# The last group of softmax weights, the last unit and the last rows in another form

## The chip, the cores and the metric

The kernel runs on one core of a Trainium2 chip. The metric is the device time of the whole launch in microseconds (us). The engines named here are TensorE (PE in the profile; PEld is its weight load), VectorE (DVE), ScalarE (ACT), GpSimd (POOL) and SyncE (SP). SP, and in this kernel ScalarE, also issue DMA transfers, which 16 DMA engines carry out. SBUF is the on-chip memory of 128 partitions; PSUM is the memory that TensorE writes.

## The reference

Eight batches of 1024 rows of 128 numbers go through one layer: a layer norm, an attention of eight query heads that share one key and one value projection, a linear "FFN", and the residual.

```
xn = _layernorm(x)                          # x: 8 x 1024 x 128, float32
Q = einsum('bnd,hdk->bhnk', xn, proj_q);  K = einsum('bmd,dk->bmk', xn, proj_k)
V = einsum('bmd,dv->bmv', xn, proj_v)
weights = softmax(einsum('bhnk,bmk->bhnm', Q, K))
Y = einsum('bhnv,hdv->bnd', einsum('bhnm,bmv->bhnv', weights, V), proj_o)
out = x + Y + sum over 8 experts of (xn @ w1[e]) @ w2[e]
```

The FFN has no activation between its two products, so the kernel folds it into one 128 x 128 matrix, `wf`.

## The kernel before

**Units and blocks.** A unit u is one head of one batch: 64 units. A unit has eight blocks of 128 queries; a block is numbered i, 0 to 511, and one pass of the main loop handles one block. The loop writes out the order on every engine by hand; no scheduler moves anything.

**One block.** `logits(i)` (L286 to L338) makes a 128 x 1024 block of logits in PSUM with four matmuls, in one of two buffers of the pool `ps_sc`; VectorE takes the row maximum (`nmax`, L335) and ScalarE the exponential with its sum (`e`, L338). `divide(i)` has VectorE take the reciprocal (L342) and ScalarE multiply (L343).

**Turning the weights.** The product with the values needs the weights with the keys on the partitions. `weights_t(i - 1)` has VectorE turn 32 x 32 squares (L365) into a tile `turned` that holds four blocks, a group. When a group is full, `move_blocks` sends its 4 x 4 pieces of 32 partitions, 128 KB each, to their partitions with 16 DMAs on SP's queue (L381). A unit has two groups, `g0` and `g1`. The last group of the last unit (blocks 508 to 511) goes another way: `weights_t_pe` transposes each block on TensorE (L354) into a `ps_sc` buffer, and ScalarE and VectorE copy one half each into `g1` (L356); nothing of it is moved by DMA.

**Seven products for eight.** The product of weights and values is done on 2 x 2 blocks (query groups by key halves) in a Strassen-Winograd form with seven products. Of the weights, x1 and x2 are the key halves of `g0`, y1 and y2 of `g1`, and four sums are made: F1 = x1 + x2 (`sum_early`, L391), then X1 = y1 - x1 (L396), X2 = F1 - y1 (L397) and F4 = y2 - X2 (L399) in `sums_late`; X1 and X2 overwrite x1 and x2 in place. All run on GpSimd, save that the last unit's `sums_late` runs on VectorE. F1 and F4 live in two alternating buffers of the tag `f`.

**Pairs.** `pair(u, j)`, j from 0 to 13, is two matmuls at L423 on the two halves of TensorE's columns, 64 wide and 512 long. Pairs 0 and 1 use x2 before it is overwritten and add to accumulator 3 (P4). Pairs 2 to 5 use y1 and y2 as they are (accumulator 0), pairs 6 to 9 use X1 and F1 (accumulator 1), pairs 10 to 13 use X2 and F4 (accumulator 2). The list `jobs` holds all pairs in order and, for each batch, four matmuls of the FFN (L446); the loop takes `PAIRS = (2, 2, 1, 2)` of them in turn from block 12 on, so the products run about a unit and a half behind the logits, and go on for 12 passes after the last block (`NS + LAG`).

**Rows.** When a batch's products are done, `collect` adds the halves of the four accumulators into `c1`, `p1`, `c2`, `y0` and `y1` (twelve steps, L478 to L504; accumulator 3 enters c1 first). For the last batch, steps 6 to 11 come behind everything else; then `rows_out_pe` transposes y0 and y1 back to rows on TensorE (L538), `finish_pe` adds x on VectorE (L542), half by half, and SP stores each half (L543).

Of the kernel before, what the change touches and what calls it, by code (L numbers as in the profile page):

```python
# [9 lines left out]
F32 = mybir.dt.float32  # L10
# [7 lines left out]
def kernel(  # L18
# [53 lines left out]
    GN = 4  # L72
# [62 lines left out]
    def scratch(tag, size, pool=work, bufs=None):  # L135
        return pool.tile([P, size], F32, tag=tag, name=f"scratch_{tag}", bufs=bufs)
# [46 lines left out]
    wqk = const.tile([P, H, P], F32, tag="wqk", name="wqk")  # L183
    wvo = const.tile([P, H, P], F32, tag="wvo", name="wvo")
    wf = const.tile([P, P], F32, tag="wf", name="wf")
    moments = const.tile([P, B, NB, 2], F32, tag="moments", name="moments")
    rstd = const.tile([P, B, NB], F32, tag="rstd", name="rstd")

# [133 lines left out]

    sums, es, turned, g0s, g1s, f1s, f4s = {}, {}, {}, {}, {}, {}, {}

    def logits(i):
        u, n = divmod(i, NB)
        pl = slot(f"pl_{i}")
        for g in range(2):  # L330
            both_halves(
                pl[:, ts(g, GS)], qTs[u][:, ts(n, P)], xnTs[u // H][:, ts(g, GS)]
            )
        nmax = small.tile([P, 1], F32, tag="nmax", name=f"nmax_{i}")
        nc.vector.reduce_max(nmax, pl, AX.X, negate=True)  # L335
        sums[i] = small.tile([P, 1], F32, tag="sums", name=f"sums_{i}")
        es[i] = work.tile([P, S], F32, tag="e", name=f"e_{i}")
        nc.scalar.activation(es[i], pl, AF.Exp, bias=nmax, accum_out=sums[i])  # L338

    def divide(i):  # L340
        rinv = small.tile([P, 1], F32, tag="rinv", name=f"rinv_{i}")
        nc.vector.reciprocal(rinv, sums.pop(i))  # L342
        nc.scalar.mul(es[i], es[i], rinv)  # L343

    def weights_t_pe(i):

        k, j = divmod(i, GN)
        u = k // 2
        if j == 0:
            g1s[u] = work.tile([P, NQ, NB, GN, Q], F32, tag="turned", name=f"g1_{u}")  # L350
        e = es.pop(i)
        pt = slot(f"pe_{i}")
        for c in range(NB):
            nc.tensor.transpose(pt[:, ts(c, P)], e[:, ts(c, P)], ident)  # L354
        for a, copy in enumerate((nc.scalar.copy, nc.vector.tensor_copy)):
            copy(  # L356
                g1s[u][:, :, ts(a, HC), j].rearrange("p r c q -> p c r q"),
                pt[:, ts(a, GS)].rearrange("p (c r q) -> p c r q", c=HC, q=Q),
            )

    def weights_t(i):
        k, j = divmod(i, GN)
        if j == 0:
# [8 lines left out]
    def move_blocks(k):  # L372
        src = turned.pop(k)
        u, g = divmod(k, 2)
        dst = work.tile(
            [P, NQ, NB, GN, Q], F32, tag=f"g{g}", name=f"g{g}_{u}", bufs=2 - g
        )
        (g1s if g else g0s)[u] = dst
        for r in range(NQ):
            for d in range(NQ):  # L380
                nc.sync.dma_start(dst[ts(d, Q), r], src[ts(r, Q), d])  # L381

    def key_half(t, a):
        return t[:, :, ts(a, HC)].rearrange("p r c t q -> p r c (t q)")
# [8 lines left out]
    def sums_late(u, engine):  # L393
        x1, x2 = key_half(g0s[u], 0), key_half(g0s[u], 1)
        y1, y2 = key_half(g1s[u], 0), key_half(g1s[u], 1)
        engine.tensor_sub(x1, y1, x1)  # L396
        engine.tensor_sub(x2, f1s[u], y1)  # L397
        f4s[u] = form("f4", u)
        engine.tensor_sub(f4s[u], y2, x2)  # L399

    accs = {}

    def pair(u, j):

        b, h = divmod(u, H)
        vf = vfs[u // GN]
        x1, x2 = key_half(g0s[u], 0), key_half(g0s[u], 1)
        if j < 2:
            acc, first, last = 3, 0, 1
            halves = ((x2, 3, j), (x2, 3, j + 2))  # L410
        else:
            acc, c = divmod(j - 2, HC)
            first, last = acc * HC + 2, acc * HC + 5
            if acc == 0:
                halves = ((key_half(g1s[u], 1), 1, c), (key_half(g1s[u], 0), 0, c))
            elif acc == 1:
                halves = ((x1, 6, c), (f1s[u], 4, c))
            else:
                halves = ((x2, 5, c), (f4s[u], 2, c))
        if h == 0 and j == first:  # L420
            accs[b, acc] = ps_acc.tile([P, GS], F32, tag=f"acc{acc}", name=f"acc{acc}_{b}")
        for half, (w, f, c) in enumerate(halves):
            nc.tensor.matmul(  # L423
                accs[b, acc][ts(half, HP)],
                lhsT=vf[:, u % GN, f, c, :],
                rhs=w[:, :, c, :],
                start=(h == 0 and j == first),
                stop=(h == H - 1 and j == last),
            )

    row_diffs, ends, ys, outs, pos = {}, {}, {}, {}, {}

    def row_diff(b):
        row_diffs[b] = late.tile([P, GS], F32, tag="diff", name=f"diff_{b}")
# [17 lines left out]
    def in_order(t):  # L454
        return t.rearrange("p (r t q) -> p t r q", r=NQ, q=Q)

    def by_query(t):
        return t.rearrange("p (t r q) -> p t r q", t=GN, q=Q)
# [70 lines left out]
            nc.sync.dma_start(r, xs[b][p, c])  # L529
        del xs[b]  # L530

    def rows_out_pe(b, g):

        if g == 0:
            pos[b] = slot(f"po_{b}")
        y = ends[b][2 + g]
        for c in range(GN):
            nc.tensor.transpose(pos[b][:, ts(g * GN + c, P)], y[:, ts(c, P)], ident)  # L538

    def finish_pe(b, g):  # L540
        c = ts(g, GN)
        nc.vector.tensor_add(xs[b][:, c], blocks(pos[b])[:, c], xs[b][:, c])  # L542
        nc.sync.dma_start(chunked(out[b])[:, c], xs[b][:, c])  # L543

# [58 lines left out]
    }  # L603

    PAIRS = (2, 2, 1, 2)
    COLLECT = {0: [0], 2: [1], 3: [2, 3], 4: [4], 6: [5], 7: [6, 7, 8], 8: [9], 10: [10], 11: [11]}

    FIRST_ROWS = 4
# [13 lines left out]
            jobs.extend((ffn, u // H, k) for k in range(2))  # L622
    jobs.reverse()

    for i in range(NS + LAG):
        m = i % GN
        if i < NS:
            logits(i)
        for task in early.get(i, ()):
            task()  # L630
        if 0 <= i - 1 < NS - GN:
            weights_t(i - 1)
        if i < NS:
            divide(i)


        v, n = divmod(i - LAG, NB)
        if n == 6 and 0 <= v + 1 < B * H:
            sum_early(v + 1)


        if i >= LAG:
            for _ in range(min(PAIRS[m] + (n == 0 and v % H == H // 2 + 1) * 2, len(jobs))):
                job, *args = jobs.pop()
                job(*args)
            if n == 0 and v < B * H:
                sums_late(v, nc.gpsimd if v + 1 < B * H else nc.vector)
        if NS - GN <= i - 1 < NS:
            weights_t_pe(i - 1)

        if i % NB == 0 and i > 0 and i // NB + 1 < B * H:
            queries(i // NB + 1)
        if i % NB == GN and i >= LAG:
            s, r = divmod(i + 20, 32)
            if s < 2 * B:
                values(s, r // NB)


        if i == 4:
            load_x(0)  # L660
        for b in range(1, B):
            r = i - FIRST_ROWS if b == 1 else i - (b - 2) * H * NB - 44
            if r in ROWS:
                ROWS[r](b)
            r = i - 20 if b == 1 else i - (b - 1) * H * NB
            if b == B - 1:
                if r == 3:
                    xn_t(b)
            elif r in (0, 4, 8, 12):
                if r == 0:  # L670
                    turn_rows(b)
                move_rows(b, r // 4)
        b, r = divmod(i - 23, H * NB)
        if r == 0 and b < B:
            row_diff(b)


        b, r = divmod(i - 69, H * NB)
        if 0 <= b < B and (b < B - 1 or r < 7):
# [12 lines left out]

    b = B - 1
    for n in (6, 7, 8, 9):
        collect(b, n)
    rows_out_pe(b, 0)
    for n in (10, 11):
        collect(b, n)
    rows_out_pe(b, 1)
    for g in range(2):  # L700
        finish_pe(b, g)
    del xs[b], pos[b], ends[b], ys[b]
    assert not jobs and not ends and not xs and not es


# [34 lines left out]
```

## Time and profile before

| what | us |
|---|---|
| median of 3 runs | 1933.43 (1933.08 to 1933.53) |
| the profiled execution, whole | 1931.35 |
| its span, first to last instruction | 1929.6 |
| PE busy in the span | 1917.4 (99%) |
| VectorE, ScalarE, GpSimd busy | 1397.4, 1358.2, 1406.3 |
| chain that ended last: PE | 87% of the span |
| matmuls of pairs, L423 (g and f, 592 ns each) | 852.2 + 490.7 busy |
| matmuls of logits, L286 pl (593 ns each) | 967.0 busy |
| moves `g<-turned`: 2032 DMAs of 128 KB | 2.4 from issue to landing |

Times of matmuls overlap, so their sum is more than the span. In a row of the timeline the first number is the start in us from the span's start, the second the duration; "x8" counts instructions, and the bracket tells how long the engine was idle before and what released it. A matmul in float32 appears as two records, so a pair is four records and a block of logits eight.

### The profile page before, as it was taken

To read this page: it belongs to the slowest core of one execution; us is meant where nothing else is said; L and a number is where in the kernel's file an instruction comes from. 1 tells how busy PE (TensorE), PEld (TensorE's weight loads), DVE (VectorE), ACT (ScalarE), POOL (GpSimd) and SP (SyncE) were. 2 spreads that over 40 slices of the span, in tenths; PEclk is the share of its full clock that TensorE was granted. 3 is DMA by queue.
4 is the path that set the end of the run, shared out by engine and by line. 5 is a ranking of instruction groups with operands and counts; after the bars stand their busy time and mean duration, and the time that the engine had idled before them with its cause. 6 is when DMAs were issued, how large, how long until landed. Compare 5 with 4: busy or idle time off the path is not lost.

```text
span 1929.6 us, 26694 instructions
## 1 busy us (share of the span) xinstructions
PE 1917.4 (99%) x8966; PEld 650.8 (34%) x8966; DVE 1397.4 (72%) x1775; ACT 1358.2 (70%) x1824; POOL 1406.3 (73%) x588
## 2 busy tenths in 40 slices
PE   9999999999999999999999999999999999999998
PEld 4433333333333333333333333333333333333333
DVE  5767778776786777777777777776777776687775
ACT  6667777777777777767777777776777776777763
POOL 2777776787777786877867778768777687677773
PEclk9999999999999999999999999999999999999999
DMA  7566666766766766677667676666765667567673
GB/s 189 131 154 153 153 139 155 158 155 155 156 153 144 172 155 149 145 159 171 142 149 156 155 171 143 156 149 149 183 143 132 149 152 169 131 148 157 144 170 82
DMA packets 137208, 292.96 MB, mean 152 GB/s; under 512 B 36464, under 2 KB 70000, under 8 KB 137072
## 3 DMA queue, kind: packets, MB, share of 16 engines
q1 hardware_dynamic: 135872, 290.67, 67.1%
q8 instruction: 72, 1.18, 0.3%
q10 hardware_dynamic: 1200, 0.59, 0.1%
q14 instruction: 64, 0.52, 0.1%
HBM read 13.76 MB, written 4.19 MB: 9 GB/s over the span
## 4 chain that ended last, share of the span: by engine, by line
PE 87%; DVE 4%; POOL 2%; ACT 2%; SPq 2%; DMA 1%; issue 1%; POOLq 0%; DVEq 0%
PE pl L286 41%; PE acc L423 34%; PE pq L286 5%; PE pv L286 5%; DVE nmax L335 2%; SPq L381 2%; ACT e L338 1%; DMA g<-turned 1%; DVE turned L365 1%; PE acc L446 1%; POOL g L396 1%; POOL g L397 1%; POOL f L399 1%; ACT e L343 1%; PE pwf L216 0%
## 5 line engine op out<-in xcount | busy, mean ns | idle before, releaser
L286 PE MATMUL pl<-xnT,qT 128*64 128x512 f32 x4096 | 967.0, 593 | 1.4 <-ACT e L338 1.0
L335 DVE TENSOR_REDUCE nmax<-pl 128x1 f32<-128x1024 f32 x512 | 626.4, 1223 | 422.1 <-PE pl L286 421.4
L338 ACT ACTIVATE e<-pl,nmax 128x1024 f32<-128x1024 f32 x512 | 570.6, 1115 | 413.6 <-DVE nmax L335 413.5
L423 PE MATMUL acc<-g,vf 128*64 128x512 f32 x2560 | 852.2, 592 | 0.0
L343 ACT ACTIVATE e<-e,rinv 128x1024 f32<-128x1024 f32 x512 | 588.1, 1149 | 115.7 <-DVE rinv L342 115.6
L365 DVE STREAM_TRANSPOSE turned<-e 128x1024 f32<-128x1024 f32 x508 | 628.7, 1238 | 10.3
L423 PE MATMUL acc<-f,vf 128*64 128x512 f32 x1024 | 490.7, 592 | 0.0
L286 PEld LDWEIGHTS pl<-xnT,qT 128*64 128x64 f32 x4096 | 291.9, 137 | 584.7 <-issue 534.4
L396 POOL TENSOR_TENSOR g<-g,g 128x2048 f32<-128x2048 f32 x63 | 287.1, 4557 | 270.3 <-DMA g<-turned 150.8
L423 PEld LDWEIGHTS acc<-g,vf 128*64 128x64 f32 x2560 | 250.5, 137 | 510.7 <-issue 506.2
L391 POOL TENSOR_TENSOR f<-g 128x2048 f32<-128x2048 f32 x64 | 291.7, 4557 | 177.6 <-PE acc L423 95.8
L399 POOL TENSOR_TENSOR f<-g,g 128x2048 f32<-128x2048 f32 x63 | 287.6, 4564 | 4.9
L397 POOL TENSOR_TENSOR g<-f,g 128x2048 f32<-128x2048 f32 x63 | 287.1, 4557 | 0.6 <-PE acc L423 0.6
L423 PEld LDWEIGHTS acc<-f,vf 128*64 128x64 f32 x1024 | 140.1, 137 | 0.0
L286 PE MATMUL pq<-xnT,wqk 128*64 128x512 f32 x512 | 121.2, 592 | 0.7 <-ACT xnT L281 0.7
L286 PE MATMUL pv<-wvo,xnT 128*64 128x512 f32 x512 | 120.9, 593 | 0.0
L342 DVE RECIPROCAL rinv<-sums 128x1 f32<-128x1 f32 x512 | 83.7, 164 | 48.3 <-ACT e L338 5.1
L338 ACT ACTIVATION_READ_ACCUMULATOR e<-pl,nmax 128x1 f32 x512 | 98.4, 192 | 0.0
L318 POOL TENSOR_TENSOR vf<-vf 128x256 f32<-128x256 f32 x64 | 47.1, 735 | 34.8 <-ACT vf L317 34.8
L298 ACT COPY qT<-pq 128x1024 f32<-128x1024 f32 (+1 forms) x66 | 63.9, 968 | 0.9 <-PE pq L286 0.7
L286 PEld LDWEIGHTS pq<-xnT,wqk 128*64 128x64 f32 x512 | 36.6, 137 | 73.0 <-issue 71.4
L286 PEld LDWEIGHTS pv<-wvo,xnT 128*64 128x64 f32 x512 | 36.4, 137 | 71.5 <-issue 69.3
(84 smaller groups left out, 529.1 us busy)
## 6 DMA issues: line engine op xcount, KB each, us to landing
g<-turned SPq DMA_DIRECT2D x2032, 128.0 KB, 2.4
xn<-in_L_attn_x_dram SPq DMA_DIRECT2D x7, 512.0 KB, 4.6
out<-yt SPq DMA_DIRECT2D x112, 32.0 KB, 1.9
x<-in_L_attn_x_dram SPq DMA_DIRECT2D x7, 512.0 KB, 4.3
xnT<-xnt SPq DMA_DIRECT2D x96, 32.0 KB, 1.9
out_dram<-x SPq DMA_DIRECT2D x6, 512.0 KB, 5.4
scratch_g<-in_L_ffn_w_dram SPq DMA_DIRECT2D x1, 2048.0 KB, 10.4
x<-in_L_attn_x_dram SPq DMA_DIRECT2D x2, 256.0 KB, 3.9
```

The lines of the kernel that those rows point to most:

```text
L286: nc.tensor.matmul(dst[r], lhsT=lhsT[:, r], rhs=rhs, start=True, stop=True)
L298: nc.scalar.copy(qTs[u][:, cols[0] * GS : (cols[-1] + 1) * GS], pq)
L335: nc.vector.reduce_max(nmax, pl, AX.X, negate=True)
L338: nc.scalar.activation(es[i], pl, AF.Exp, bias=nmax, accum_out=sums[i])
L342: nc.vector.reciprocal(rinv, sums.pop(i))
L343: nc.scalar.mul(es[i], es[i], rinv)
L365: nc.vector.transpose(turned[k].rearrange("p k c t q -> p c k t q")[:, :, :, j, :], es.pop(i).rearrange("p (c k q) -> p c k q", k=NQ, q=Q),)
L391: nc.gpsimd.tensor_add(f1s[u], key_half(g0s[u], 0), key_half(g0s[u], 1))
L396: engine.tensor_sub(x1, y1, x1)
L397: engine.tensor_sub(x2, f1s[u], y1)
L399: engine.tensor_sub(f4s[u], y2, x2)
L423: nc.tensor.matmul(accs[b, acc][ts(half, HP)], lhsT=vf[:, u % GN, f, c, :], rhs=w[:, :, c, :], start=(h == 0 and j == first), stop=(h == H ...
```

## The change

- The last group (blocks 508 to 511) is turned by VectorE like all others, and `weights_t_pe` is gone. Its 16 moves are issued half by ScalarE's queue and half by SP's, alternating by the destination; they go into a free buffer of the tag `vf` instead of a `g1` buffer.
- In the last four passes of the loop `PAIRS_LAST = (2, 1, 1, 0)` takes four pairs in place of seven: three pairs come after the last logits instead of between them. The loop ends with the last block; the rest of the pairs of unit 62 follow it.
- The last unit's pairs run in the order 0, 2 to 5, 6 to 9, 10 to 13, 1. So that x2 is still there for pair 1, the last unit's X2 goes into a buffer of its own (`f2s`, in a `g0` buffer).
- The last batch's rows are put together by `last_rows` in an order of its own, with accumulators 0 to 2 alone: two copies on ScalarE and eight adds on VectorE. Accumulator 3 (P4) is copied to SBUF by ScalarE (`d4`) and added on TensorE: the rows are transposed by plain matmuls with the identity, and for the first four chunks a second matmul adds P4's two halves with `fold`, two 64 x 64 identities one above the other. `fold` is made by two GpSimd copies at the start.
- The second half of the last store is issued on ScalarE's queue.

```diff
+    fold = const.tile([P, HP], F32, tag="fold", name="fold")
+    for half in (lo, hi):
+        nc.gpsimd.tensor_copy(fold[half], ident[half, half])
...
-    def weights_t_pe(i):
...
     def move_blocks(k):
         src = turned.pop(k)
         u, g = divmod(k, 2)
-        dst = work.tile(
-            [P, NQ, NB, GN, Q], F32, tag=f"g{g}", name=f"g{g}_{u}", bufs=2 - g
-        )
+        queues = (nc.sync,)
+        if k < 2 * B * H - 1:
...
+        else:
+            queues = nc.scalar, nc.sync
+            dst = scratch("vf", VF, batch)[:, :TURNED].rearrange(
+                "p (r c t q) -> p r c t q", r=NQ, c=NB, q=Q
+            )
         (g1s if g else g0s)[u] = dst
         for r in range(NQ):
             for d in range(NQ):
-                nc.sync.dma_start(dst[ts(d, Q), r], src[ts(r, Q), d])
+                queues[d % len(queues)].dma_start(dst[ts(d, Q), r], src[ts(r, Q), d])
...
     def sums_late(u, engine):
...
+        f2s[u] = x2
+        if u == B * H - 1:
+            f2s[u] = scratch("g0", TURNED)[:, : TURNED // 2].rearrange(
+                "p (r c x) -> p r c x", r=NQ, c=HC
+            )
         engine.tensor_sub(x1, y1, x1)
-        engine.tensor_sub(x2, f1s[u], y1)
+        engine.tensor_sub(f2s[u], f1s[u], y1)
         f4s[u] = form("f4", u)
-        engine.tensor_sub(f4s[u], y2, x2)
+        engine.tensor_sub(f4s[u], y2, f2s[u])
...
+    def last_rows(b, jobs):
...
+        run(0, 1)
+        run(2, 6)
+        nc.scalar.copy(p1[lo], bot(0))
+        nc.scalar.copy(p1[hi], bot(0))
+        add(y1[lo], top(0), p1[lo])
+        run(6, 10)
+        add(c1[lo], top(1), p1[lo])
+        add(c1[hi], bot(1), p1[hi])
+        add(c2[hi], top(1), c1[hi])
+        run(10, 14)
+        add(y0[hi], top(2), c2[hi])
+        add(y0[lo], top(2), c1[lo])
+        add(y1[hi], bot(2), c1[hi])
+        add(y1[hi], top(2), y1[hi])
+        run(1, 2)
+        nc.scalar.copy(by_query(d4), in_order(accs[b, 3]))
+        po = slot(f"po_{b}")
+        ys = tiles[1]
+        for c in range(NB):
+            x_rows = c < GN
+            nc.tensor.matmul(
+                po[:, ts(c, P)], lhsT=ys[:, ts(c, P)], rhs=ident, start=True, stop=not x_rows
+            )
+            if x_rows:
+                nc.tensor.matmul(
+                    po[:, c * P : c * P + HP],
+                    lhsT=d4[:, ts(c, P)],
+                    rhs=fold,
+                    start=False,
+                    stop=True,
+                )
+        for g, queue in enumerate((nc.sync, nc.scalar)):
+            c = ts(g, GN)
+            add(xs[b][:, c], blocks(po)[:, c], xs[b][:, c])
+            queue.dma_start(chunked(out[b])[:, c], xs[b][:, c])
...
     PAIRS = (2, 2, 1, 2)
+    PAIRS_LAST = (2, 1, 1, 0)
...
-    for i in range(NS + LAG):
+    for i in range(NS):
...
-        if 0 <= i - 1 < NS - GN:
+        if 0 <= i - 1:
             weights_t(i - 1)
...
-            for _ in range(min(PAIRS[m] + (n == 0 and v % H == H // 2 + 1) * 2, len(jobs))):
+            pairs = (PAIRS if i < NS - GN else PAIRS_LAST)[m]
+            for _ in range(pairs + (n == 0 and v % H == H // 2 + 1) * 2):
...
-        if NS - GN <= i - 1 < NS:
-            weights_t_pe(i - 1)
...
+    weights_t(NS - 1)
+    sum_early(B * H - 1)
+    while len(jobs) > 14:
+        job, *args = jobs.pop()
+        job(*args)
+    sums_late(B * H - 1, nc.vector)
+    last_rows(B - 1, jobs[::-1])
```

More of the change, by code (lines that the diff above doesn't have):

```diff
@@ L321, in values @@
         nc.gpsimd.tensor_sub(t4, b21, t2)
-    sums, es, turned, g0s, g1s, f1s, f4s = {}, {}, {}, {}, {}, {}, {}
+    sums, es, turned, g0s, g1s, f1s, f2s, f4s = {}, {}, {}, {}, {}, {}, {}, {}
     def logits(i):
@@ L343, in divide @@
         nc.scalar.mul(es[i], es[i], rinv)
-    def weights_t_pe(i):
[L347 to L358, printed above, removed]
-            )
     def weights_t(i):
@@ L374, in move_blocks @@
         u, g = divmod(k, 2)
-        dst = work.tile(
-            [P, NQ, NB, GN, Q], F32, tag=f"g{g}", name=f"g{g}_{u}", bufs=2 - g
-        )
+        queues = (nc.sync,)
+        if k < 2 * B * H - 1:
+            dst = work.tile(
+                [P, NQ, NB, GN, Q], F32, tag=f"g{g}", name=f"g{g}_{u}", bufs=2 - g
+            )
[4 more added lines that the diff above has]
+            )
         (g1s if g else g0s)[u] = dst
@@ L418, in pair @@
             else:
-                halves = ((x2, 5, c), (f4s[u], 2, c))
+                halves = ((f2s[u], 5, c), (f4s[u], 2, c))
         if h == 0 and j == first:
@@ L429, in pair @@
             )
-    row_diffs, ends, ys, outs, pos = {}, {}, {}, {}, {}
+    row_diffs, ends, ys, outs = {}, {}, {}, {}
     def row_diff(b):
@@ L530, in store, with top, bot, run @@
         del xs[b]
[L532 to L543, printed above, removed]
+    def last_rows(b, jobs):
+        add = nc.vector.tensor_add
+        tiles = [rows_tile(f"end{k}_{b}").rearrange("p a b -> p (a b)") for k in range(2)]
+        p1, c1, y0, y1 = (by_query(t[:, ts(k, GS)]) for t in tiles for k in range(2))
+        c2 = by_query(late.tile([P, GS], F32, tag="end", name=f"end_{b}"))
+        d4 = late.tile([P, GS], F32, tag="diff", name=f"d4_{b}")
+        def top(k):
+            return in_order(accs[b, k][lo])
+        def bot(k):
+            return in_order(accs[b, k][hi])
+        def run(first, last):
+            for job, *args in jobs[first:last]:
+                job(*args)
[29 more added lines that the diff above has]
+                    stop=True,
+                )
+        for g, queue in enumerate((nc.sync, nc.scalar)):
+            c = ts(g, GN)
+            add(xs[b][:, c], blocks(po)[:, c], xs[b][:, c])
+            queue.dma_start(chunked(out[b])[:, c], xs[b][:, c])
     def one(t):
@@ L623 @@
     jobs.reverse()
-    for i in range(NS + LAG):
+    for i in range(NS):
         m = i % GN
-        if i < NS:
-            logits(i)
+        logits(i)
         for task in early.get(i, ()):
             task()
-        if 0 <= i - 1 < NS - GN:
+        if 0 <= i - 1:
             weights_t(i - 1)
-        if i < NS:
-            divide(i)
+        divide(i)
         v, n = divmod(i - LAG, NB)
-        if n == 6 and 0 <= v + 1 < B * H:
+        if n == 6 and v + 1 >= 0:
             sum_early(v + 1)
         if i >= LAG:
-            for _ in range(min(PAIRS[m] + (n == 0 and v % H == H // 2 + 1) * 2, len(jobs))):
+            pairs = (PAIRS if i < NS - GN else PAIRS_LAST)[m]
+            for _ in range(pairs + (n == 0 and v % H == H // 2 + 1) * 2):
                 job, *args = jobs.pop()
                 job(*args)
-            if n == 0 and v < B * H:
-                sums_late(v, nc.gpsimd if v + 1 < B * H else nc.vector)
-        if NS - GN <= i - 1 < NS:
-            weights_t_pe(i - 1)
+            if n == 0:
+                sums_late(v, nc.gpsimd)
         if i % NB == 0 and i > 0 and i // NB + 1 < B * H:
@@ L678 @@
         b, r = divmod(i - 69, H * NB)
-        if 0 <= b < B and (b < B - 1 or r < 7):
+        if 0 <= b:
             for n in COLLECT.get(r, ()):
@@ L691 @@
                 load_x(b + 1)
[L693 to L703, printed above, removed]
+    weights_t(NS - 1)
+    sum_early(B * H - 1)
+    while len(jobs) > 14:
+        job, *args = jobs.pop()
+        job(*args)
+    sums_late(B * H - 1, nc.vector)
+    last_rows(B - 1, jobs[::-1])
+    del xs[B - 1]
+    assert not ends and not xs and not es
 _INS = [
```

## The prediction

> **What bounds the kernel now.** The page comes first: TensorE is busy 99% of the span and holds 87% of the chain that ended last. The change touches only the last four of 512 softmax blocks, so what it is worth is read from the last 45 us, in the timeline (start, us, engine, line, operation, what ended the idle time before it). Two rows set the pace while blocks are still made:
>
> ```profile
> 1881.22 1.11 ACT L338 ACTIVATE e<-pl,nmax 128x1024 f32<-128x1024 f32 x1 [0.85 <-DVE nmax L335]
> 1883.80 1.11 ACT L338 ACTIVATE e<-pl,nmax 128x1024 f32<-128x1024 f32 x1
> ```
>
> With one pair between logits, a block takes 1883.80 - 1881.22 = 2.58 us, and the second row has no idle before it: ScalarE is full. With two pairs TensorE sets 3.44 us: four units of 0.86 us, two for the logits and one for each pair (the chain's "1.72 PE acc L423 x8" is two pairs). At the end the page's picture changes:
>
> ```profile
> 1891.01 1.09 PE L354 MATMUL pe<-ident,e 128*128 128x128 f32 x8
> 1905.10 0.69 DVE L356 COPY g<-pe 128x512 f32<-128x512 f32 x1 [0.75 <-ACT g L356]
> 1905.54 4.53 POOL L391 TENSOR_TENSOR f<-g 128x2048 f32<-128x2048 f32 x1 [3.31 <-PE acc L423]
> 1910.10 2.29 DVE L396 TENSOR_TENSOR g<-g,g 128x2048 f32<-128x2048 f32 x1 [4.32 <-POOL f L391]
> 1920.31 0.59 PE L423 MATMUL acc<-f,vf 128*64 128x512 f32 x1
> 1921.11 0.68 DVE L498 TENSOR_TENSOR end<-acc,end 64x512 f32<-64x512 f32 x1
> 1924.70 1.29 DVE L542 TENSOR_TENSOR x<-po,x 128x512 f32<-128x512 f32 x2 [0.75 <-PE po L538]
> ```
>
> The last group's weights are in place at 1905.8 (second row). The last unit's F1, on GpSimd, starts late because it waits for TensorE; from there the chain is F1, three VectorE sums, ten adds, four transposes, two adds, store. VectorE leaves L396 to L504 with hardly a gap, and TensorE's last pair (slot 1920.31 to 1920.74) is close behind: both bind.
>
> The third view is windows of the same stretch (busy of PE, PEld, DVE, ACT, POOL, then granted clock, DMA share, GB/s), for the transfers of the group before the last and for the end:
>
> ```profile
> 1892.00:1894.00 2.00, 2.00 (x11) 0.77 (x12) 0.31 (x2) 1.62 (x2) 2.00 (x2) 1.00 0.91 203
> 1894.00:1896.00 2.00, 1.85 (x12) 0.86 (x8) 1.58 (x2) 0.39 (x1) 2.00 (x1) 1.00 0.92 211
> 1896.00:1898.00 2.00, 1.13 (x6) 0.48 (x8) 0.17 (x1) 1.77 (x3) 1.92 (x2) 1.00 0.95 209
> ...
> 1925.00:1926.00 1.00, 0.00 (x0) 0.00 (x0) 0.99 (x2) 0.00 (x0) 0.00 (x0) 1.00 0.00 0
> 1926.00:1927.00 1.00, 0.00 (x0) 0.00 (x0) 0.00 (x0) 0.00 (x0) 0.00 (x0) 0.69 0.63 172
> 1927.00:1928.00 1.00, 0.00 (x0) 0.00 (x0) 0.00 (x0) 0.00 (x0) 0.00 (x0) 0.50 1.04 293
> ```
>
> While one queue moves a group, the 16 DMA engines are already over 90% busy at some 207 GB/s. And the clock halves at about 1926.4: 1.7 us after the last transposes, 5.5 us after the last pair.
>
> **Part by part.** *Turning by VectorE.* It takes four groups of eight transposes (4 x 1.09 us) off TensorE and four half copies each off ScalarE (0.57 us) and VectorE (0.69 us), and frees the logits' two buffers, which the transposes shared. The three pairs taken out from between the logits shorten each step to ScalarE's 2.58 us. The third block from the end keeps its row: exponential at 1890.67. Then 1893.25 and 1895.83; exponential start to end of the division is 2.59 us (1881.22 to 1883.81): 1898.42. VectorE's turn (1.24 us a block, L365) ends at **1899.7**; the three turns before it lie in VectorE's idle time. Last logits start at 1892.6 instead of 1896.9.
>
> *Moving.* Turned weights now have to cross partitions: 16 moves of 128 KB. For the group before, the turn ended at 1888.36 (L365 at 1887.12), and GpSimd's wait for the landing ended at 1900.3 (chain rows of L391): 11.9 us, 16 issues 0.64 us apart, a first packet 1.2 us after the turn and a landing at the end. Two queues would help if the 0.64 us were the queue's issue (an issue of the final store takes 0.39 us on SP); but the share of 0.91 to 0.95 says that the engines are the limit. The Trainium skill speaks against the change here ("DMA: Bandwidth & Descriptors", section "Rules for kernel authors"): queues on several engines share the same 16 DMA engines, so that only issue time is saved. By the issue row alone two queues would need 8 x 0.64 = 5.1 us less; by the share, at most 5% of 10.2, 0.5 us. I take nothing. In the order of the changed program ScalarE's last four moves each wait for its first four to land, and several of SP's for ScalarE's; six moves (3.8 us) are in flight at first, so I take no gap, at worst 1 us. Behind these waits on ScalarE stand only the two P1 copies, which are not due. Weights land at 1899.7 + 11.9 = **1911.6**, 5.8 us later than now.
>
> *TensorE up to there.* Logits end at 1894.35. Six pairs of the unit before: 1899.5. The last four need its F4, the third of GpSimd's sums after 1888.57 (L396, L397, L399: 3 x 4.55): 1902.25. That is 2.6 us of waiting, then about 1905.5; one pair of the last unit (its own X2 needs only the first group): 1906.4. Then nothing to do until 1911.6: **5.2 us idle**. F1 follows F4 on GpSimd, 1902.3 to 1906.8, so it is off the chain; what is late next is the move.
>
> *From the landing.* Four pairs with the weights themselves 1911.7 to 1915.1; X1 on VectorE 1911.7 to 1914.0, X2 and F4 done after 2.21 + 2.29 more and start-up, as now 1910.10 to 1916.92, 6.82 us: 1918.5. Pairs 6 to 9 to 1918.6, pairs 10 to 13 to 1922.0. The new buffer for X2, which allows the late second pair, waits for the unit before (1905.5): free. P1's copies and four adds (0.71 us apart) fall into the last four pairs.
>
> *The end.* After pair 13 two adds for y0; meanwhile the late pair (0.86), then the P4 copy (0.58, as L204's 128x512): 1.7 us after the slot's end. Then plain fp32 matmuls instead of transposes: nearest row L216, 16 records for 8 matmuls in 1.95 us, 0.22 each, twice the transposes' 0.11. Eight (y0 and P4) last until 3.5, hiding y1's two adds (3.05); four more 4.5; two adds of x, 1.29 together: 5.8 us. Today the same stretch is 1920.74 to 1925.99, 5.25. So two P4 adds off VectorE buy nothing, as P4's matmuls stand on the path: +0.6. The second store on ScalarE's queue saves no time: its add comes 0.6 us after the first, SP's issue is 0.39. The two copies for `fold` lie in GpSimd's idle first slice (page: 2 tenths); uncovered some 0.4 us.
>
> Sum at full clock: 1922.0 + 5.8 - 1925.99 = **+1.8 us**.
>
> *The clock.* 5.2 us of idle TensorE is where row and rule part. By the row the clock fell 5.5 us after the last pair, if transposes don't count as work: 5.2 us would just hold, +1.8. By the Trainium skill ("TensorE: Matmul & The Clock Gate", section "What's actually happening") activity is judged in free-running windows of 3.4 us; one idle window halves the clock, one busy window restores it. An idle of 5.2 us holds a whole window in (5.2 - 3.4)/3.4, about half of the phases, and a mostly idle one in more. I take the rule: the drop comes up to 2 us before the landing, and the clock returns at the next window's end. Pairs run at half speed for 2 to 3.4 us, losing half: 1 to 1.7, an estimate from that page; I take 1.6. Bounds: 0, and 2.8 (two windows). Total **+3.4 us**. On the profiled execution's own 1931.35 that is 1934.75; the runs' median is 1933.43, so **1936.8**. A measurement can tell 0.2%, 3.9 us, from no change: the forecast is a little slower, within it.
>
> **Rivals.** *The clock holds*: phase of the windows, or the lone pair at 1906 counts; +1.8, 1935.2. For it: the row of 5.5 us. *The clock stays at half for two windows* (the side of slower): if it drops early in the gap, the next window is still half idle and doesn't restore it; the first matmuls of the kernel (from 1.31) also ran slow (two 128x512 records of L567 take 2.08 us there, two of L208 take 1.12 at 46.59). It decides from about 5.5 us of half clock: 2.8 us, total +4.6, 1938.0; past 1937.3 this is slower by over 0.2%. *Two queues do move faster*: if 0.64 us is issue, the weights land at 1906.5, F1 (1906.8) is late next, there is no idle gap: 1.8 - 4.8 = -3.0, 1930.4. Against it: the 0.91 to 0.95.
>
> **Chances.** Forecast 0.50, clock holds 0.27, two windows 0.15, faster moves 0.08. The forecast's spread (2.4 to 4.6) has some 0.35 above 3.9; with most of the two-window case, slower is 0.33; faster by over 3.9 us needs more than the best rival: 0.02. The range leaves out the faster moves and a tail above: 1933.6 (landing 0.6 us earlier, less at the end, no drop) to 1938.9 (two windows and 1 us of gaps in the moves).
>
> **What would show it.** Turn ending near 1899.7; landing 11 to 12 us on, share above 0.9; TensorE idle from about 1906.4 to 1911.6; windows after it below clock 1.00; after pair 13 some 5.8 us to the last add. Wrong: a landing before 1908, logits bound by something other than ScalarE's 2.58 us, or a clock of 1.00 throughout.

## The result, and the profile after

| | us | runs |
|---|---|---|
| before, beside it | 1932.78 (1931.19 to 1933.53) | 22 |
| changed | 1935.68 (1933.33 to 1938.16) | 22 |
| ratio | 1.0014, 95% interval 1.0008 to 1.002 | |
| profiled execution before, changed | 1931.35, 1935.21 | |
| span before, changed | 1929.6, 1933.3 | |

The changed kernel is 2.9 us slower (1.5 to 3.9 by the interval): measurable here, but inside the 0.2% that the forecast called no change. Its runs spread over 4.8 us, those of before over 2.3. Five of all the executions reported below took 2540 to 6907 us and are left out of the medians.

The timeline of the changed kernel shows the steps of the sum (start, us, engine, line, operation, in brackets the idle time before it and what ended that):

```profile
1890.56 1.11 ACT L341 ACTIVATE e<-pl,nmax 128x1024 f32<-128x1024 f32 x1 [0.85 <-DVE nmax L338]
1893.14 1.11 ACT L341 ACTIVATE e<-pl,nmax 128x1024 f32<-128x1024 f32 x1
1895.71 1.11 ACT L341 ACTIVATE e<-pl,nmax 128x1024 f32<-128x1024 f32 x1
1898.33 1.25 DVE L352 STREAM_TRANSPOSE turned<-e 128x1024 f32<-128x1024 f32 x1 [1.21 <-ACT e L346]
1899.60 9.85 SPq L375 DMA_DIRECT2D scratch_vf<-turned  x8
1899.65 6.21 ACTq L375 DMA_DIRECT2D scratch_vf<-turned  x8
1902.26 4.52 POOL L385 TENSOR_TENSOR f<-g 128x2048 f32<-128x2048 f32 x1
1902.36 1.07 PE L422 MATMUL acc<-f,vf 128*64 128x512 f32 x1 [1.96 <-POOL f L398]
...
1906.68 0.59 PE L422 MATMUL acc<-f,vf 128*64 128x512 f32 x1
...
1911.64 2.29 DVE L395 TENSOR_TENSOR g<-scratch_vf,g 128x2048 f32<-128x2048 f32 x1 [12.06 <-DMA scratch_vf<-turned]
1911.68 5.35 PE L422 MATMUL acc<-scratch_vf,vf 128*64 128x512 f32 x16 [3.12 <-DMA scratch_vf<-turned]
...
1924.85 0.58 ACT L564 COPY d<-acc 128x512 f32<-128x512 f32 x1 [6.61 <-PE acc L422]
...
1928.41 1.29 DVE L582 TENSOR_TENSOR x<-po,x 128x512 f32<-128x512 f32 x2 [1.65 <-PE po L569]
```

The three exponentials are 2.58 us apart: ScalarE sets the pace of the last blocks. The last turn ends at 1899.58, and VectorE's first sum (L395) starts 12.06 us later; the bracket names the moves. F1 (L385) had been done since 1906.8, so nothing else was awaited. Where before this sum started at 1910.10 behind GpSimd, it now starts at 1911.64 behind DMA. At the end the adds of x finish at 1928.41 + 1.29 = 1929.70, against 1925.99 before: 3.7 of the 3.9 us between the two profiled executions are there already.

A matmul of a pair takes 1.07 us at 1902.36 and 0.59 at 1906.68: the same work at two clocks. The windows view says so directly (length, busy us of PE, PEld, DVE, ACT, POOL, then granted clock, share of the DMA engines, GB/s):

```profile
1900.00:1902.00 2.00, 0.41 (x1) 0.00 (x0) 0.00 (x0) 0.00 (x0) 2.00 (x1) 1.00 0.63 131
1902.00:1904.00 2.00, 1.64 (x4) 0.50 (x6) 0.00 (x0) 0.00 (x0) 2.00 (x2) 0.61 0.99 199
1904.00:1906.00 2.00, 2.00 (x8) 0.66 (x6) 0.00 (x0) 0.00 (x0) 2.00 (x1) 0.54 0.86 225
1906.00:1908.00 2.00, 2.00 (x10) 0.56 (x6) 0.00 (x0) 0.00 (x0) 0.78 (x1) 1.00 0.86 217
1908.00:1910.00 2.00, 0.56 (x2) 0.00 (x0) 0.00 (x0) 0.00 (x0) 0.00 (x0) 1.00 0.91 211
1910.00:1912.00 2.00, 0.32 (x2) 0.23 (x4) 0.36 (x1) 0.00 (x0) 0.00 (x0) 1.00 0.32 66
1912.00:1913.00 1.00, 1.00 (x6) 0.35 (x4) 1.00 (x1) 0.00 (x0) 0.00 (x0) 0.84 0.06 16
1913.00:1914.00 1.00, 1.00 (x4) 0.30 (x2) 1.00 (x2) 0.00 (x0) 0.00 (x0) 0.50 0.00 0
1914.00:1915.00 1.00, 1.00 (x5) 0.31 (x3) 1.00 (x1) 0.00 (x0) 0.00 (x0) 0.50 0.00 0
1915.00:1916.00 1.00, 1.00 (x6) 0.45 (x4) 1.00 (x1) 0.00 (x0) 0.00 (x0) 0.50 0.00 0
1916.00:1917.00 1.00, 1.00 (x8) 0.49 (x6) 0.90 (x2) 0.00 (x0) 0.00 (x0) 0.95 0.00 0
```

The clock falls twice, from 1902.44 to 1905.85 and from 1912.68 to 1916.09 by its records, 3.41 us each time. The first drop lies ahead of a wait and, by these rows, only shortens it. The second meets pairs that have nothing to wait for: 3.41 us at half speed lose 1.7.

### The profile page after: what moved, and what is told of

It reads as the page before. It is cut to its first block, busy times and chain, and to the rows that moved or that the text cites. A ratio compares the mean times of both kernels' runs of the same rounds, so it can differ in the third digit from the quotient of the medians.

```text
span 1933.3 us, 26679 instructions
## 1 busy us (share of the span) xinstructions
PE 1918.5 (99%) x8950; PEld 651.2 (34%) x8950; DVE 1398.2 (72%) x1773; ACT 1355.7 (70%) x1820; POOL 1406.1 (73%) x590
## 4 chain that ended last, share of the span: by engine, by line
PE 88%; DVE 3%; POOL 3%; ACT 2%; SPq 2%; DMA 1%; issue 1%; ACTq 0%; DVEq 0%; POOLq 0%
PE pl L289 41%; PE acc L422 35%; PE pv L289 5%; PE pq L289 5%; SPq L375 2%; DVE nmax L338 2%; ACT e L341 1%; DVE turned L352 1%; DMA g<-turned 1%; POOL f L398 1%; POOL g L395 1%; POOL g L396 1%; PE acc L445 1%; ACT e L346 1%; PE pwf L219 0%
## 5 line engine op out<-in xcount | busy, mean ns | idle before, releaser
L352 DVE STREAM_TRANSPOSE turned<-e 128x1024 f32<-128x1024 f32 x512 | 633.8, 1238 | 11.7 <-ACT e L346 1.2
L395 POOL TENSOR_TENSOR g<-g,g 128x2048 f32<-128x2048 f32 x63 | 287.1, 4558 | 274.6 <-DMA g<-turned 147.4
L385 POOL TENSOR_TENSOR f<-g 128x2048 f32<-128x2048 f32 x64 | 291.7, 4558 | 170.6 <-PE acc L422 88.5
```

Source lines behind the costliest of these rows:

```text
L352: nc.vector.transpose(turned[k].rearrange("p k c t q -> p c k t q")[:, :, :, j, :], es.pop(i).rearrange("p (c k q) -> p c k q", k=NQ, q=Q),)
L385: nc.gpsimd.tensor_add(f1s[u], key_half(g0s[u], 0), key_half(g0s[u], 1))
```

## The experiments

Medians in us, each beside runs of the kernel before on the same chip. "Over before" is the difference of these medians; the interval belongs to the ratio of the runs.

| kernel | median (runs) | over before | ratio, 95% interval |
|---|---|---|---|
| changed | 1935.68 (22) | +2.9 | 1.0014, 1.0008 to 1.002 |
| gaps filled (`fill_both`) | 1934.64 (21) | +1.6 | 1.0009, 1.0003 to 1.0016 |
| second gap filled (`fill_late`) | 1935.19 (21) | +2.2 | 1.0012, 1.0005 to 1.0019 |
| one queue (`one_queue`) | 1936.79 (12) | +3.8 | 1.0022, 1.0013 to 1.003 |
| queues on different halves (`halves`) | 1935.24 (19) | +2.2 | 1.0014, 1.0007 to 1.002 |
| the same, starting together (`halves_wait`) | 1935.21 (21) | +2.4 | 1.0015, 1.0008 to 1.0021 |
| old pairs (`old_pairs`) | 1937.02 (12) | +4.2 | 1.0021, 1.0013 to 1.003 |
| old order and rows (`old_rows`) | 1935.87 (21) | +3.0 | 1.0017, 1.001 to 1.0023 |
| TensorE turns, new pairs (`pe_turn`) | 1939.16 (6) | +6.3 | 1.0032, 1.002 to 1.0043 |
| TensorE turns, old pairs (`pe_turn_old_pairs`) | 1934.56 (20) | +2.4 | 1.001, 1.0003 to 1.0017 |
| TensorE turns, full (`pe_turn_full`) | 1932.73 (13) | +0.5 | 1.0, 0.9992 to 1.0008 |
| half of the moves left out (`half_move`) | 1932.85 (13) | +0.7 | 1.0001, 0.9993 to 1.0009 |
| half by TensorE, half moved (`half_half`) | 1930.89 (13) | -2.0 | 0.9992, 0.9984 to 1.0 |

### The clock

`fill_both` puts matmuls whose results nothing reads into both gaps of TensorE, so that it does not rest:

```diff
+    def fill(n):
+        t = slot(f"fill_{n}")
+        for _ in range(n):
+            nc.tensor.matmul(t[:, :GS], lhsT=ident, rhs=wqk[:, :GN, :], start=True, stop=True)
...
     while len(jobs) > 14:
+        if len(jobs) == 18:
+            fill(2)
...
         run(0, 1)
+        fill(5)
         run(2, 6)
```

> Changed kernel, with matmuls of no use (2 of 128x512 while TensorE waits for the unit before's F4, 5 while it waits for the moved weights). My theory: with the clock held, 1.7 us per dropped window come back. Granted clock 1.00 up to the last matmul, landing unchanged at 11.9 us after the last turn, median about 2.0 us above the kernel before (the changed kernel stood 2.9 above), and a spread of runs of under 3 us instead of 4.8. Rival (the idle time costs nothing beyond the wait): median stays 2.9 us above, spread as wide as now.

Measured: +1.6 us. Its windows, the same columns as above:

```profile
1904.00:1906.00 2.00, 2.00 (x11) 1.08 (x8) 0.00 (x0) 0.00 (x0) 2.00 (x1) 1.00 0.78 205
1908.00:1910.00 2.00, 2.00 (x6) 0.92 (x5) 0.00 (x0) 0.00 (x0) 0.00 (x0) 1.00 0.93 209
1914.00:1916.00 2.00, 2.00 (x12) 0.86 (x10) 2.00 (x2) 0.46 (x1) 0.00 (x0) 1.00 0.00 0
```

The clock is 1.00 where the changed kernel had 0.54 and 0.50, the landing is the same 12.06 us behind the turn, and the runs spread over 2.3 us instead of 4.8. The record gives each run's mean granted clock as well (it counts a fall behind the last matmul too, which costs nothing): all 21 runs stand at 1.000 here, while of the changed kernel's runs 8 stand at 0.999, with a median of 1934.05, and 14 at 0.998, with 1936.12. So the idle gaps are what lowers the clock, and by the medians the drop is worth 2.9 - 1.6 = 1.3 us (the intervals of the two ratios overlap, so the size is rough). What remains, +1.6, is the loss at full clock.

`fill_late` has `fill(4)` in the second gap only.

> The same with the second filling alone (4 matmuls). My theory: the half clock of the first gap (1902.4 to 1905.9 in the profile) is hidden by the wait for the moved weights, so within 0.4 us of the kernel with both fillings, 2.0 us above the kernel before. Rival: the first drop counts too, 2.5 us or more above.

Measured: +2.2; its interval overlaps that of `fill_both` and that of the changed kernel. In its profile the clock stayed at 1.00 through the first gap too, with nothing put into it, so that execution says nothing on what a first drop costs. Its runs say a little more: seven stand at a mean clock of 1.000, with a median of 1934.28, and fourteen at 0.999, with 1935.58. Most of them probably had a drop, then, and those were 1.3 us slower; whether it was the first one, which would speak for the rival, or one that the four matmuls did not prevent, is not on record. That the first drop is hidden is read from the changed kernel's rows (TensorE is idle again after it), not shown by this pair.

### The moves

`one_queue` sends all 16 moves through SP.

```diff
-            queues = nc.scalar, nc.sync
+            queues = (nc.sync,)
```

> Changed kernel, all 16 moves of the last group on SP's queue. My theory (the DMA engines are the limit): landing 11.9 us after the last turn, as with two queues, time within 0.5 us of the changed kernel. Rival (two queues save issue time): landing later by 2 us or more, and the time up by as much.

Measured: +3.8. The timeline:

```profile
1900.27 10.02 SPq L375 DMA_DIRECT2D scratch_vf<-turned  x16
...
1912.59 2.29 DVE L395 TENSOR_TENSOR g<-scratch_vf,g 128x2048 f32<-128x2048 f32 x1 [12.34 <-DMA scratch_vf<-turned]
```

12.34 us of waiting against 12.06: the second queue buys 0.3 us of landing. The time is 0.9 above the changed kernel's, with overlapping intervals; in this profile the clock was at half for 6.83 us, from 1909.91 to 1916.74, 4.2 of them behind the landing.

`halves` keeps two queues, but lets one read partitions 0 to 63 and write 64 to 127 while the other does the opposite; the changed kernel's two queues read the same quarter.

```diff
-        for r in range(NQ):
+        for r in range(NQ // 2):
             for d in range(NQ):
-                queues[d % len(queues)].dma_start(dst[ts(d, Q), r], src[ts(r, Q), d])
+                for a, queue in enumerate(queues):
+                    s, e = r + a * NQ // 2, (d + a * NQ // 2) % NQ
+                    queue.dma_start(dst[ts(e, Q), s], src[ts(s, Q), e])
```

> Changed kernel, with two queues that read different halves of the partitions: ScalarE's queue takes sources 0 to 63 and SP's 64 to 127, destinations opposite. If a move of 32 partitions is held by the SBUF ports of its half (packets of 4 KB take 0.29 us), packets shorten towards 0.16 us, landing comes about 10 us after the turn, and the time falls about 2 us against the changed kernel: about 1 us above the kernel before. If the limit is the DMA engines themselves, packets stay at 0.29 us, landing at 11.9. If the waits of one queue for the other are the limit, packets shorten but the landing stays within 0.5 us of 11.9.

Measured: +2.2, the landing 11.58 us behind the turn (which ended at 1900.58). The windows:

```profile
1902.00:1903.00 1.00, 0.00 (x0) 0.00 (x0) 0.00 (x0) 0.00 (x0) 1.00 (x1) 1.00 0.94 299
1902.50:1903.00 0.50, 0.00 (x0) 0.00 (x0) 0.00 (x0) 0.00 (x0) 0.50 (x1) 1.00 1.02 402
1903.00:1904.00 1.00, 0.86 (x4) 0.34 (x6) 0.00 (x0) 0.00 (x0) 1.00 (x2) 1.00 0.85 225
1904.00:1906.00 2.00, 2.00 (x12) 0.72 (x10) 0.00 (x0) 0.00 (x0) 2.00 (x1) 1.00 0.90 199
```

For half a us, with both queues at work, the engines carried 402 GB/s at a share of 1.02, with packets of 0.16 us; from 1904 they are back at 199 GB/s and a share of 0.90, with packets of about 0.3. So a high share does not mean that the engines can do no more: a 4 KB packet of 0.3 us is stretched by something else. Different halves are not the only place of short packets. In the changed kernel's trace they took 0.16 us from about 1904.5 to 1905.5 too, with ScalarE's queue alone at work, and over that us the engines carried no more than one queue does otherwise, 209 GB/s on average:

```profile
1904.50:1905.00 0.50, 0.50 (x4) 0.07 (x2) 0.00 (x0) 0.00 (x0) 0.50 (x1) 0.50 0.64 246
1905.00:1905.50 0.50, 0.50 (x4) 0.17 (x2) 0.00 (x0) 0.00 (x0) 0.50 (x1) 0.50 0.57 172
```

In `halves` the fast stretch ended when SP's moves waited for ScalarE's to land and one queue was left.

`halves_wait` tries to keep both going: ScalarE starts its moves only when the group before has landed.

```diff
+        nc.scalar.copy(warm, g0s[u][:, NQ - 1, 0, 0, :1])
         for r in range(NQ // 2):
```

> As the kernel with the halves, but ScalarE first copies one column of the last unit's g0 (128x1), so that its moves come behind the landing of the group before and the waits of SP's moves are for SP's own. Theory of the ports (packets of 4 KB take 0.16 us while the two queues read and write different halves, 0.29 otherwise, as in the 1 us in which the halves kernel had both going): landing 7 to 8 us after the last turn, nearly no idle before it, time 1.5 to 2.3 us below the kernel before. Rival (the 16 DMA engines carry no more than 207 GB/s for long): landing still 11 us or later, time as the changed kernel's.

Measured: +2.4, landing 11.89 us behind the turn. Packets took 0.16 us for 0.7 us only, then 0.29 to 0.33 with both queues active. That misses what the theory of the halves expected; what stretches a packet when both queues run on stays open.

`half_move` leaves half of the last group's moves out (source quarters 2 and 3) and copies in place of them, so the last unit's products are not the reference's.

```diff
+        n = NQ // len(queues)
+        if n < NQ:
+            nc.vector.tensor_copy(dst[:, n:], src[:, n:])
-        for r in range(NQ):
+        for r in range(n):
```

> The changed kernel with half of the last group's moves left out: sources 0 and 1 are moved, a copy in place on VectorE stands for the other half (so the last unit's products are not the reference's). Theory (the 16 moves set the landing; 8 of them take half of the 10.2 us): landing 6 to 7.5 us after the last turn, that is near 1906.5; F1, which GpSimd ends near 1906.8, is late next; TensorE has no gap of 3 us after it; time 1 to 3 us below the kernel before, that is 4 to 6 us below the changed kernel. Rival (something behind the landing holds the end as well): less than 2 us below the changed kernel.

Measured: +0.7, that is 2.2 us below the changed kernel by the distances to before: between the two theories. The timeline says why:

```profile
1896.48 7.92 SPq L378 DMA_DIRECT2D g<-turned  x5
...
1900.92 2.51 ACTq L378 DMA_DIRECT2D scratch_vf<-turned  x4
...
1906.66 4.52 POOL L388 TENSOR_TENSOR f<-g 128x2048 f32<-128x2048 f32 x1 [2.89 <-DMA scratch_vf<-turned]
...
1911.21 2.29 DVE L398 TENSOR_TENSOR g<-scratch_vf,g 128x2048 f32<-128x2048 f32 x1 [6.36 <-POOL f L388]
```

The last packet of the moves ended 7.5 us after the turn's end at 1900.84 and their completion came 7.9 us after it (11.7 in the changed kernel by the same measure), and the sum now waits for F1 (last bracket), as theory said. But F1 itself started 2.9 us late: two moves of the group before stood on SP's queue until 1903.3, behind completions of ScalarE's moves, and F1 needs them. The loss by the moves is shown, its full size not, as a new wait took part of it.

### Parts undone

`old_pairs` restores `PAIRS_LAST = (2, 2, 1, 2)` with VectorE turning.

> Changed kernel with the three pairs left between the last logits (2, 2, 1, 2). My theory: ScalarE's 2.58 us sets these steps but for one, so that the last turn is 0.9 us later, and the landing and the end with it: 0.9 us above the changed kernel. Rival (the move is not on the path): no change.

Measured: +4.2, 1.3 above the changed kernel; the last turn ends at 1902.03, and the landing comes 12.09 us after it. With VectorE turning, the faster pace of the last logits is a gain, as the last turn starts the moves. How much of the 1.3 us is the pace is not shown: the intervals overlap, and in this profile the clock was at half from 1911.74 to 1918.57, 4.4 us of it behind the landing, against 3.4 in the changed kernel's.

`old_rows` restores the order of the last unit's pairs and the rows as before: pairs 0 and 1 first, P4 added by VectorE, transposes instead of plain matmuls.

```diff
-        run(0, 1)
+        run(0, 2)
         run(2, 6)
+        nc.scalar.copy(c1[lo], bot(3))
...
+        add(c1[lo], top(3), c1[lo])
...
-        run(1, 2)
-        nc.scalar.copy(by_query(d4), in_order(accs[b, 3]))
...
+            nc.tensor.transpose(po[:, ts(c, P)], ys[:, ts(c, P)], ident)
```

> Changed kernel with pairs 0 and 1 of the last unit first and P4 added by VectorE, rows by TensorE's transposes; all else as changed. My theory: P4 on TensorE is worth nothing either way: the last pair is 0.86 us earlier and the stretch behind pair 13 shorter by 0.6 the one way, two adds more the other; within 0.6 us of the changed kernel. Rival (P4's matmuls are the loss): 1 us or more below the changed kernel.

Measured: +3.0, the same as the changed kernel. Its timeline, from the landing to the last add:

```profile
1912.83 2.29 DVE L395 TENSOR_TENSOR g<-scratch_vf,g 128x2048 f32<-128x2048 f32 x1 [12.09 <-DMA scratch_vf<-turned]
...
1929.43 1.29 DVE L571 TENSOR_TENSOR x<-po,x 128x512 f32<-128x512 f32 x2 [0.75 <-PE po L568]
```

That takes 17.9 us, against 18.1 in the changed kernel (1911.64 to 1929.70). But here the clock was at half from 1910.98 to 1917.81, 5.0 us of it behind the landing, in which pairs that waited for nothing lost 2.5; in the changed kernel they lost 1.7. Less these losses, 15.4 stand against 16.4 (`fill_both`, at full clock, takes 16.4 from 1911.81 to 1928.20). So by the traces the late pair and P4 on TensorE cost about 1.0 us, an estimate from two executions, and the equal medians hide it behind the clock.

`pe_turn` keeps everything new but lets TensorE turn the last group, with `weights_t_pe` as before.

```diff
-        if 0 <= i - 1:
+        if 0 <= i - 1 < NS - GN:
             weights_t(i - 1)
...
+        if NS - GN <= i - 1:
+            weights_t_pe(i - 1)
...
-    weights_t(NS - 1)
+    weights_t_pe(NS - 1)
```

> Changed kernel with the last group turned by TensorE and copied, as before the change; pairs, their order and the last rows as changed. My theory (the move of the last group is the loss): weights in place by 1906 again, no drop of the clock, within 0.6 us of the kernel before. Rival (the new order or P4 on TensorE is the loss): stays 2 us or more above the kernel before.

Measured: +6.3, which was not expected. Its timeline:

```profile
1896.26 1.22 DVE L338 TENSOR_REDUCE nmax<-pl 128x1 f32<-128x1024 f32 x1
1901.20 1.21 DVE L338 TENSOR_REDUCE nmax<-pl 128x1 f32<-128x1024 f32 x1
...
1913.22 4.52 POOL L401 TENSOR_TENSOR f<-g 128x2048 f32<-128x2048 f32 x1 [8.50 <-PE acc L438]
1917.77 2.29 DVE L411 TENSOR_TENSOR g<-g,g 128x2048 f32<-128x2048 f32 x1 [9.97 <-POOL f L401]
```

The row maxima of the last two blocks are 4.94 us apart: transposes and logits share two buffers, and a block costs that with one pair or with two (before the change the maxima stand at 1889.41, 1894.37 and 1899.31, with two pairs in the first step and one in the second). The pairs that had filled this wait now come behind it; F1 needs a buffer that they still read, starts at 1913.22 behind them (8.50 idle) instead of 1905.54, and the sums start at 1917.77. A part of the 6.3 us is the clock's again: TensorE stands idle from 1902.43 to 1905.09 by its records, and in the window from 1906 to 1908 its clock is 0.50. The three later pairs are right only together with VectorE's turning.

`pe_turn_old_pairs` is `pe_turn` with (2, 2, 1, 2).

> TensorE turns the last group as before the change, the seven pairs stand between the last logits as before (2, 2, 1, 2); the new order of the last unit and the new rows stay. Theory (with TensorE turning, moving three pairs behind the logits is what cost over 3 us in the run that kept the new pairs; the order and the rows are worth nothing): within 0.7 us of the kernel before, the weights complete near 1905.5, clock 1.00 to the last pair. Rival (the new order or the new rows carry the loss): 2 us or more above the kernel before.

Measured: +2.4, the ratio's interval from +0.6 to +3.3 us. The pairs' place, together with the drop of the clock seen there (all of these runs stand at a mean clock of 1.000, those of `pe_turn` at 0.998 and 0.999), explains 3.9 of the 6.3. The rest is not gone: it stands with the new order, the new rows and where F1 finds its buffer, and these runs do not tell which. No profile of this kernel is used.

### Versions that might beat both

`pe_turn_full` fills TensorE's waits with one more pair and gives the last F1 a buffer of its own; four chunks of the rows go back to transposes.

```diff
-    PAIRS_LAST = (2, 1, 1, 0)
+    PAIRS_LAST = (2, 2, 2, 2)
...
+        f1s[u] = (
+            scratch("vf", VF, batch)[:, : TURNED // 2].rearrange("p (r c x) -> p r c x", r=NQ, c=HC)
+            if u == B * H - 1
+            else form("f1", u)
+        )
```

> TensorE turns the last group, eight pairs between the last logits (2, 2, 2, 2), so that its waits for the buffers of the logits are full; the last unit's F1 has a buffer of its own, so that GpSimd makes it right behind F4 (done near 1906.8 instead of 1910.07); new order and new rows, with transposes again for the four chunks without P4. Theory (before, the end hung on F1 and on TensorE's queue of pairs together; with F1 earlier the sums start near 1907 and only TensorE's work is left): 1 to 2 us below the kernel before. Rival (TensorE's work alone sets the end before, F1 is hidden): within 0.5 us of the kernel before.

Measured: ratio 1.0 (0.9992 to 1.0008): the rival. F1 was indeed earlier, yet the last add comes no sooner:

```profile
1904.02 4.53 POOL L405 TENSOR_TENSOR scratch_vf<-g 128x2048 f32<-128x2048 f32 x1
...
1908.58 2.29 DVE L415 TENSOR_TENSOR g<-g,g 128x2048 f32<-128x2048 f32 x1 [1.61 <-POOL scratch_vf L405]
...
1926.10 1.29 DVE L604 TENSOR_TENSOR x<-po,x 128x512 f32<-128x512 f32 x2 [1.15 <-PE po L590]
```

Blocks run 1.3 us later in this profile than in that of before (the exponential of 1896.94 there stands at 1895.62). Less that, the sum starts at 1907.3 instead of 1910.10, and the last add ends at 1926.1, where before ended at 1925.99: In the kernel before TensorE has no gap over 0.25 us from 1896.87 to the end of its last pair at 1920.90, so its own work sets that end, and F1 was hidden. This version differs from `pe_turn_old_pairs` by one more pair, F1's buffer and the four transposes, and is 1.8 us faster by the distances to before; which of the three does it was not run.

`half_half` gives each way half of the work. VectorE turns all four blocks, but SP moves only query quarters 0 and 1, eight moves; quarters 2 and 3 are transposed by TensorE behind the last logits and copied by ScalarE. Two of the last blocks get buffers of their own, to live that long.

```diff
+        for r in range(NQ if k < 2 * B * H - 1 else NQ // 2):
...
+    def half_turn(i):
+        j = i % GN
+        pt = slot(f"pe_{i}")[:, :GS]
+        e = last_es[i]
+        for c in range(NB):
+            nc.tensor.transpose(pt[:, ts(c, HP)], e[hi, ts(c, P)], ident[hi, hi])
+        nc.scalar.copy(
+            g1s[B * H - 1][:, NQ // 2 :, :, j].rearrange("p r c q -> p c r q"),
+            pt.rearrange("p (c r q) -> p c r q", c=NB, q=Q),
+        )
...
+    half_turn(NS - 4)
+    half_turn(NS - 3)
     while len(jobs) > 14:
+        if len(jobs) == 18:
+            half_turn(NS - 2)
+            half_turn(NS - 1)
```

> The changed kernel, with half of the last group's weights (query quarters 0 and 1 of each block) turned by VectorE and moved by SP in 8 moves, and the other half transposed by TensorE behind the last logits and copied by ScalarE; transposes again for the four chunks without P4. Theory (the 16 moves and the gap they leave are the loss; the logits' faster pace is a gain): landing 6.4 to 7.5 us after the last turn (5.1 us less than 16 moves), about when GpSimd ends F1 (1906.8 in the changed kernel's profile); TensorE without an idle stretch over 1.5 us in its place, clock 1.00 until the pairs are done; 1 to 3 us below the kernel before. Rival (F1 or TensorE's own work sets the same end as before whatever is moved): within 0.7 us of the kernel before. What would make it worse: transposes of 64 rows that take as long as those of 128, 4.4 us in all.

Measured: 2.0 us below before; the interval just reaches 1.0. Eleven of its 13 runs took 1929.6 to 1931.4, all at a mean clock of 1.000; the other two took 1934.4 and 1934.6, at 0.998. The profile caught one of these two:

```profile
1900.00:1902.00 2.00, 2.00 (x6) 0.60 (x8) 1.25 (x1) 1.07 (x3) 2.00 (x1) 0.50 0.66 146
1902.00:1904.00 2.00, 2.00 (x6) 0.47 (x4) 0.00 (x0) 0.00 (x0) 2.00 (x1) 0.50 0.71 156
```

and in its timeline

```profile
1896.22 0.71 PE L386 MATMUL pe<-ident,e 64*128 64x64 f32 x8
...
1907.38 0.59 PE L437 MATMUL acc<-f,vf 128*64 128x512 f32 x1
1907.90 1.21 PE L386 MATMUL pe<-ident,e 64*128 64x64 f32 x16
1908.07 4.53 POOL L400 TENSOR_TENSOR f<-g 128x2048 f32<-128x2048 f32 x1 [3.70 <-DMA scratch_vf<-turned]
```

Here TensorE did little but the transposes between 1896.2 and 1898.8, the clock was at half from 1898.62 to 1905.44, and the pairs that read the buffer which F1 needs ended at 1907.97; F1 follows at once, 3.7 us late (the bracket names the moves, whose last packet ended at 1907.90, but F1 does not read them, and their completion came only at 1908.24). That is 6.8 us after the turn, as expected. A lower clock at the wrong place costs this version its gain, and a filled gap may keep it; that was not run.

## Why the prediction was right

**The turn and the pace.** Forecast 1899.7, measured 1899.58; 2.58 us a block, measured 2.58 and 2.57. `old_pairs` shows the other side: without the faster pace the time rises by up to 1.3 more.

**The moves.** Forecast 11.9 us from turn to landing, measured 12.06, and without the second queue 12.34. The 0.5 us allowed for two queues bounds the 0.3 they bring. The conclusion held, but its reason did not: the share above 0.9 was read as "the engines are the limit", and the 402 GB/s at 1.02 in `halves` show that the share can be filled by stretched packets. The last row of the prediction's own windows, 293 GB/s at 1.04 in the final store, already spoke against it. The predicted waits of ScalarE's and SP's moves for each other are there: SP's third move of the last group starts at 1905.76 by the trace, yet the windows show 225 and 217 GB/s meanwhile, so they leave no gap, as assumed.

**The first wait for F4.** Forecast to 1902.25, measured 1902.36.

**The idle gap.** Here a step was off: forecast 1906.4 to 1911.6, 5.2 us; measured 1907.97 to 1911.68, 3.7 us. The sum had no drop of the clock after the first wait of 2.5 us. It costs nothing in itself by these rows, as the landing is awaited anyway. Where the first wait left the clock at 1.00, the gap is longer: by the records' ends it is 3.12 us in the changed kernel's profile (the bracket at 1911.68), but 5.24 in that of `one_queue` and 4.59 in that of `halves`.

**The clock.** By the row of before (5.5 us without pairs until the fall) 3.7 us would have been safe, and +1.8 the answer. By the Trainium skill's windows ("TensorE: Matmul & The Clock Gate", section "What's actually happening") of 3.4 us, one of which must be idle, a gap of 3.7 us would drop the clock in (3.7 - 3.4)/3.4, about a tenth of the phases, an estimate from that page's figure. The drop came all the same. Its length agrees with the page, 3.41 us, but the window ahead of it held records for 29% of the time: a window need not be idle. So 1.6 us came out right, 1.7 in the profiled execution and 1.3 in the median by `fill_both`, with a gap taken too long and a condition taken too strict, and that is partly luck.

**The end.** Forecast 5.8 us from pair 13 to the last add, measured 1923.7 to 1929.70, 6.0. In `old_rows` the same stretch took 5.1 us (1925.66 to 1930.72), so the new rows cost 0.9 us where 0.6 were forecast.

**The sum.** +1.8 at full clock was forecast, +1.6 measured with the clock held up. With the clock +3.4 forecast, +2.9 measured. The forecast of 1936.8 stood on a median before of 1933.43; beside the changed kernel's runs it was 1932.78, which is the other half of the 1.1 us between forecast and result. The rival of faster moves is refuted by 12.06; the one of two windows came true in the profiles of five variants (`one_queue`, `halves`, `halves_wait`, `old_pairs`, `old_rows`: 6.83 us at half clock around the landing), not in that of the changed kernel. How many of its other runs had it is not on record: two single drops and one of two windows give the same mean clock, 0.998.

## What to carry to other kernels

When an operation is moved from a full engine to DMA at the end of a kernel, nothing runs beside the transfer any more: count the time from the last instruction to the landing, and then what the emptied engine does in it. An idle gap of TensorE can cost twice, once as waiting and once as half clock behind it; fill it with throwaway matmuls before judging the rest. Half by each way can beat either way alone, where both are limited by different things (2.0 us here, with an interval that just reaches no change); and two edits that look separate (who turns, and when the pairs run) can each be wrong without the other.

## What was not expected of the hardware

- **A window that is only partly idle lowers the clock.** In the changed kernel's trace the 3.41 us ahead of the two drops held TensorE records for 43% and 29% of the time. Before the change, 5.6 us passed from the last pair to the drop, with transposes between, and the last 3.41 of them held records for 28%. In five variants (`one_queue`, `halves`, `halves_wait`, `old_pairs`, `old_rows`) such a stretch, around the first wait, held 46 to 51%, and the clock stayed at 1.00. Only `half_half` falls out of line, where 50% (1.7 us, 0.7 of them in transposes of 64 rows) lowered it. The ends of matmul records are modelled, so these shares are rough.
- **The share of the DMA engines is not what they can carry.** 4 KB packets took about 0.3 us at a share of 0.9 and some 207 GB/s, and 0.16 us at 402 GB/s for half a us while two queues worked on different halves of the partitions. They also took 0.16 us with one queue at work, at 209 GB/s on average and a share of 0.6, so short packets alone move no more; what stretches the others stays open.
- **The start moves.** The trace's first record of full clock stands at 8.0 us in one profile and at 14.8 in another, for the same work; with it the last turn's end moves from 1899.58 (8.04) to 1900.74 (`old_rows`, 13.17), though both do the same up to there. A shift of 1 us between two single profiles is therefore no finding: the changed kernel (8.04) and the one before (8.09) can be compared directly.
